# Edge messages of a graph network in batches of five tiles instead of four, with begun sums made at one go

## The chip, the cores and the metric

The kernel runs on one core of a Trainium2 chip. The metric is the device time of one execution in microseconds (us). The core has five engines that run side by side, each through its own list of instructions in order: TensorE (PE; its weight loads are shown apart as PEld), VectorE (DVE), ScalarE (ACT), GpSimd (POOL) and SyncE (SP, which issues transfers). Matmuls write to PSUM, eight banks of 512 floats in each of 128 partitions; everything else works in the larger SBUF.

## What is computed

One block of a graph network on 1250 nodes of 512 floats (three vector components of 128 channels and 128 scalars) with 40000 edges, a residual and a layernorm:

```python
s_j = silu(x[src][:, 384:] @ W1 + b1) @ W3 + b3
edge_basis = rbf(r) * cutoff(r) @ W2 + b2          # 20 radial functions of the edge's length
s1, s2, s3 = split(s_j * edge_basis)
v_msg = v_j * s1[:, :, None] + s3[:, :, None] * edge_attr1[:, None, :]
x = x + segment_sum(concat(v_msg, s2), dst)        # first half
v, dot, s1, s3 = per_node(x, U, V, Wu1, Wu2)      # norms and a small network
x = x + segment_sum(concat(v * s1, dot + s3)[src], dst)   # second half
out = layernorm(x_in + x)
```

The edges come sorted by destination; source rows have to be gathered.

## The kernel before, in words

The nodes form NB = 10 blocks of 128 rows. A first part (to about 38 us) loads everything, runs the first two layers for each node and writes a table of 640 floats per node to DRAM (`table1`). Then follows the edge loop, in which nearly all the time goes.

**Tiles and batches.** 40000 edges are 79 chunks of 512, and each chunk has four tiles of 128 edges. Four chunks make a group `g` (20 groups); a batch is tile `i` of each of the four chunks of a group. So there are NT = 80 batches: 76 of four tiles, then of 3, 2, 2 and 2, 313 tiles in all. The loop runs over steps `t`, one batch each.

**A step.** DVE runs `messages(t)`: two multiplies of the gathered rows by the edge factors, in place (L938, on 4 x 256 elements, and L940, on 4 x 384), then `make_hot` (L870: a one-hot matrix of destinations) and `make_spread` (L881: the same times the edge's direction), and `make_pair` (L958, for the count of links). Both hot and spread read four columns that the factors' matmul carries along, so L881 is the last reader of the factor banks. PE adds the messages of the batch before (`add_messages(t - 1)`, L974 and L980, 4 + 12 matmuls), counts its links (`count_links`, L1003), and makes the factors of the next batch (`edge_factors(t + 1)`, L928). Each tile's factors are a matmul over 25 rows at row 32 j of the array, j being the tile's chunk in the group; the trace shows two per tile. They go to `eb`, one set of four PSUM banks, which is made new only when L881 has read the last factors. POOL runs `gather(t + 3)` (L769), one indirect DMA of 128 rows for each tile, the first of them behind `edge_factors(t + 1)` by a dependency put there by hand. The rows have five rooms of four tiles, taken in turn: three in the tile that the profile calls `more`, two in `nodes`.

**Second half.** The other work is hung between these steps by tables: `first`, `early`, `late`, `mid`, `dve` and `amid` list tasks by step and rank, and `run(when, step)` issues them at fixed places of the step: `early` on PE ahead of the next factors, `late` behind them, `amid` on DVE ahead of the pair, `dve` at the step's end. Every eight steps or so two groups close, and a block of nodes passes through its second half with short products that all use one PSUM bank, `work` (`ps_work`, one buffer). The second segment sum uses a matrix of link counts (`cast`) and the finished rows, split in two parts (`upper`, `lower`). As rows of early blocks are there long before the last, ten partial sums ("chains", `begin_out`, L1378) and a last one are begun during the loop in a bank of their own, `begun`: from step 24 on, one pair of products at a time, in slots of `early` and `late`, then copied by ACT (L1397) and sent to DRAM. So the eight banks are four of `eb`, and `work`, `agg`, `adj` and `begun`. After the loop the sums are completed and normalized.

The schedule is manual: instructions run on each engine in the order in which the code issues them.

Of the kernel before, what the change touches and what calls it, by code (L numbers as in the profile page):

```python
# [21 lines left out]
P = 128  # L22
C = 128
# [23 lines left out]
PACK = 4096.0  # L47

# [16 lines left out]
def gnn_resnorm(  # L65
# [43 lines left out]
    )  # L109
    sh.n_nodes, sh.width, sh.n_edges, sh.NB, sh.tail = n_nodes, width, n_edges, NB, tail  # L110
# [40 lines left out]
    def load(engine, ap, shape, name):  # L151
        t = const.tile(shape, F32, name=name)
        engine.dma_start(t, ap)
        return t
# [15 lines left out]
    sh.nodes = const.tile([P, NB * width], F32, name="nodes")  # L170
# [14 lines left out]
    size = CPG * (V + 2 * C)  # L185
    sh.more = const.tile([P, 3 * size], F32, name="more")
# [14 lines left out]
    sh.w1_sb = load(nc.sync, w1, [C, C], "w1_sb")  # L201
# [9 lines left out]
    sh.w3_sb = load(nc.sync, w3, [C, V], "w3_sb")  # L211
# [407 lines left out]
def windowed(tc, sh):  # L619
# [36 lines left out]
    NT = len(batches)  # L656

# [3 lines left out]
    def runs(g, i):  # L661

        out = []
        for j in tiles(g, i):
            if out and lanes(g, i, out[-1][-1]) == lanes(g, i, j):
                out[-1].append(j)
            else:
                out.append([j])
        return [(slice(js[0], js[-1] + 1), len(js), lanes(g, i, js[0])) for js in out]

# [12 lines left out]
    with tc.tile_pool(  # L683
# [5 lines left out]
        turn = pool.tile([P, 2, EPG, N_RBF], F32, name="turn", bufs=1)  # L689
        upper, lower = (  # L690
            pool.tile([P, NB, width], F32R, name=name, bufs=1) for name in ("upper", "lower")
        )

# [67 lines left out]
        rooms = itertools.cycle(sh.rooms)  # L761

        def gather(t, behind=None):

            g, i = batches[t]
            rows_t = next(rooms)
            for j in tiles(g, i):
                n = lanes(g, i, j)
                got = nc.gpsimd.indirect_dma_start(  # L769
                    out=rows_t[:n, j, :],  # L770
# [3 lines left out]
                        ap=sh.src_i[:n, g, i * CPG + j : i * CPG + j + 1], axis=0  # L774
                    ),
                )
                if behind is not None and j == 0:
# [4 lines left out]
            clear_rest(t, rows_t, nc.gpsimd)  # L782
            rows_of[t] = rows_t
# [63 lines left out]
        def clear_rest(t, tile, engine=nc.vector):  # L847
            g, i = batches[t]
            for j in tiles(g, i):
                m = lanes(g, i, j)  # L850
                if m < P:
                    engine.memset(tile[m:, j], 0.0)

        def carried(t, js, m):

            g, i = batches[t]
            if g == 0:
                return sh.carried[:m, g, i * CPG + js.start : i * CPG + js.stop, :]
            return factors_of(t, js)[:m, :, V : V + CARRY]

        def make_hot(t):

            g, i = batches[t]
            hots[t] = pool.tile([P, CPG, WIN], F32, name="hot", bufs=3)
            spread[t] = pool.tile([P, CPG, 3, WIN], F32, name="spread", bufs=3)
            clear_rest(t, hots[t])
            clear_rest(t, spread[t])
            for js, n, m in runs(g, i):
                shape = [m, n, WIN]
                nc.vector.tensor_tensor(  # L870
                    hots[t][:m, js, :],
                    lane[:m, None, :WIN].to_broadcast(shape),
                    carried(t, js, m)[:, :, 3:].to_broadcast(shape),
# [3 lines left out]
        def make_spread(t):  # L877
            g, i = batches[t]
            for js, n, m in runs(g, i):
                shape = [m, n, 3, WIN]  # L880
                nc.vector.tensor_mul(  # L881
                    spread[t][:m, js],
                    hots[t][:m, js, None, :].to_broadcast(shape),
                    carried(t, js, m)[:, :, :3, None].to_broadcast(shape),
                )
# [23 lines left out]
        made_in = {}  # L909
# [10 lines left out]
        def factors_of(t, js):  # L920

            return made_in[t][:, js]

        def edge_factors(t):
            g, i = batches[t]
            for j in tiles(g, i):
                rows = slice(j * FEAT, j * FEAT + N_RBF + 1 + CARRY)
                made = nc.tensor.matmul(  # L928
                    made_in[t][:, j, : V + CARRY], turned[g][rows, i, :], sh.w2_sb[rows, :],
# [4 lines left out]
        def messages(t):  # L934
            g, i = batches[t]
            msg = rows_of.pop(t)
            for js, n, m in runs(g, i):
                nc.vector.tensor_mul(msg[:m, js, V:], msg[:m, js, V:], factors_of(t, js)[:m, :, C:V])  # L938
            for js, n, m in runs(g, i):
                nc.vector.tensor_mul(  # L940
                    msg[:m, js, :V].rearrange("p t (k c) -> p t k c", k=3),
                    msg[:m, js, :V].rearrange("p t (k c) -> p t k c", k=3),
                    factors_of(t, js)[:m, :, None, :C].to_broadcast([m, n, 3, C]),
                )
            make_hot(t)
            make_spread(t)
            run(amid, t)
            make_pair(t)
            msgs[t] = msg
# [18 lines left out]
        def add_messages(t):  # L968
# [3 lines left out]
            agg, msg, js = aggs[g], msgs.pop(t), tiles(g, i)  # L972
            for j in js:
                nc.tensor.matmul(  # L974
                    agg[j * WIN : (j + 1) * WIN, :], hots[t][:, j, :],
                    msg[:, j, :width], start=(i == 0), stop=False, skip_group_check=True,
                )
            for c in range(3):
                for j in js:
# [1194 lines left out]
```

## Time and profile before

| | |
|---|---|
| runs | 478.65, 477.8, 480.88 us (median 478.65) |
| profiled execution | 480.96 us, of which the span of the trace is 479.2 |
| mean granted TensorE clock | 0.957 |
| busy: PE, DVE, ACT, POOL | 402.6, 427.8, 375.3, 334.9 us |
| first gather starts, last gather starts | 26.35, 426.96 us |

Times in the trace are microseconds from the start of the span. A row of a group gives the line, the engine and operation, the tile written and those read, partitions x elements of each, the count, and behind the bar the busy time, the mean in ns and the engine's idle time before these instructions with what ended it. "issue" is idle time in which the engine waited for nothing that the profile shows. A row of the timeline gives the start, the duration, and in brackets the idle time before it and its releaser; neighbours of one kind are drawn together (x8). A row of a window gives its length and the busy time and count for PE, PEld, DVE, ACT and POOL, then the granted clock, the DMA share and GB/s.

### The profile page before, as it was taken

Reading aid. Unit: us, or ns where it says so; the run is one execution under the profiler, and the core shown is the slowest. Engines: PE = TensorE matmul, PEld = TensorE weight load, DVE = VectorE, ACT = ScalarE, POOL = GpSimd, SP = SyncE. Lnnn points to the kernel's source line nnn. Section 1 sums busy time; section 2 is a strip of 40 time slices with the busy share of each in tenths; the row PEclk is TensorE's granted clock in tenths of the full one; section 3 lists DMA queues with packets and bytes.
Section 4 is the critical chain, followed back from the end, with each engine's and each line's share of the span. In section 5 each row is a group of like instructions: output and inputs, shape, how many; then the busy total and the mean of one; then the engine's idle time right before and its main releaser. Section 6 shows DMA issues by size and latency. Waiting matters only on the chain. (4 is left out here: it accounts for less than half of the span.)

```text
span 479.2 us, 11259 instructions
## 1 busy us (share of the span) xinstructions
PE 402.6 (84%) x4259; PEld 229.3 (48%) x4259; DVE 427.8 (89%) x675; ACT 375.3 (78%) x971; POOL 334.9 (70%) x364
## 2 busy tenths in 40 slices
PE   8645586878879778798889888989999999999992
PEld 6322243445445345444435544555555655555782
DVE  6569899999999899999999999999999999978584
ACT  4377846689869968877977897799899889967672
POOL 9267777777777777777777777777777777771530
PEclk9857979899999999989989999999999999999998
DMA  8887888788888888888888988888888888879024
GB/s 238 301 247 253 254 265 271 240 279 262 281 254 272 289 259 275 270 269 255 280 276 255 293 267 280 266 291 287 287 275 293 265 284 291 280 242 319 4 71 151
DMA packets 37810, 123.29 MB, mean 257 GB/s; under 512 B 7124, under 2 KB 9782, under 8 KB 37746
## 3 DMA queue, kind: packets, MB, share of 16 engines
q0 software_dynamic: 25568, 104.34, 69.0%
q1 hardware_dynamic: 10834, 17.35, 10.6%
q10 hardware_dynamic: 1344, 0.79, 0.5%
q8 instruction: 35, 0.57, 0.5%
q14 instruction: 29, 0.24, 0.2%
HBM read 112.94 MB, written 9.51 MB: 256 GB/s over the span
## 5 line engine op out<-in xcount | busy, mean ns | idle before, releaser
L769 POOL DMA_INDIRECT more<-table,src_i x189 | 184.6, 977 | 66.3 <-issue 48.1
L769 POOL DMA_INDIRECT nodes<-table,src_i x124 | 119.8, 966 | 37.8 <-issue 33.2
L903 ACT ACTIVATE one<-one,weight,src_f 128x128 f16<-128x128 f16 x313 | 128.5, 482 | 0.2
L928 PE MATMUL eb<-w_sb,basis_t 25*128 25x388 f32 x614 | 74.1, 551 | 54.3 <-DVE spread L881 43.9
L893 ACT ACTIVATE one<-number,low 128x128 f16<-128x128 f16 x313 | 99.8, 392 | 11.2 <-PE adj L1003 11.2
L940 DVE TENSOR_TENSOR more<-more,eb 128x1536 f32<-128x1536 f32 (+2 forms) x48 | 81.8, 1705 | 0.0
L938 DVE TENSOR_TENSOR more<-more,eb 128x1024 f32<-128x1024 f32 (+2 forms) x48 | 57.0, 1190 | 15.0 <-PE eb L928 8.2
L928 PEld LDWEIGHTS eb<-w_sb,basis_t 25*128 25x128 f32 x614 | 24.7, 187 | 76.5 <-DVE spread L881 63.7
L974 PE MATMUL agg<-more,hot 128*32 128x512 f32 x378 | 52.8, 624 | 0.0
L940 DVE TENSOR_TENSOR nodes<-nodes,eb 128x1536 f32<-128x1536 f32 x30 | 52.4, 1747 | 0.0
L980 PEld LDWEIGHTS agg<-more,spread 128*32 128x32 f32 x1134 | 33.5, 111 | 30.2 <-issue 29.6
L938 DVE TENSOR_TENSOR nodes<-nodes,eb 128x1024 f32<-128x1024 f32 x30 | 36.5, 1216 | 6.9 <-PE eb L928 4.0
L881 DVE TENSOR_TENSOR spread<-hot,eb 128x384 f32<-128x384 f32 (+1 forms) x74 | 40.4, 547 | 2.5
L980 PE MATMUL agg<-more,spread 128*32 128x128 f32 x1134 | 40.2, 273 | 0.0
L958 DVE TENSOR_TENSOR pair<-number,column 128x640 f16<-128x640 f16 (+1 forms) x81 | 38.5, 476 | 0.0
L1003 PE MATMUL adj<-pair,one 128*128 128x160 f16 x313 | 35.4, 235 | 0.3 <-DVE basis L827 0.3
L974 PE MATMUL agg<-nodes,hot 128*32 128x512 f32 x248 | 34.9, 619 | 0.0
L980 PEld LDWEIGHTS agg<-nodes,spread 128*32 128x32 f32 x744 | 22.7, 112 | 20.0 <-issue 19.6
L1003 PEld LDWEIGHTS <-one 128*128 128x128 f16 x313 | 21.6, 100 | 16.0 <-issue 13.5
L845 ACT COPY basis_t<-work 128x512 f32<-128x512 f32 x20 | 11.6, 580 | 22.5 <-PE work L840 22.5
L1378 PE MATMUL begun<-upper,cast 128*128 128x512 f32 x57 | 27.8, 487 | 0.0
L980 PE MATMUL agg<-nodes,spread 128*32 128x128 f32 x744 | 27.5, 277 | 0.0
(299 smaller groups left out, 697.3 us busy)
## 6 DMA issues: line engine op xcount, KB each, us to landing
table<-more SPq DMA_DIRECT2D x10, 320.0 KB
more<-table,src_i POOLq DMA_INDIRECT x189, 4.2
spilled<-begun SPq DMA_DIRECT2D x10, 256.0 KB
more<-spilled SPq DMA_DIRECT2D x2, 1280.0 KB
node_x<-in_x_dram SPq DMA_DIRECT2D x35, 64.0 KB
nodes<-table,src_i POOLq DMA_INDIRECT x124, 4.2
out_dram<-more SPq DMA_DIRECT2D x7, 256.0 KB
nodes<-in_x_dram POOLq DMA_DIRECT2D x2, 768.0 KB
```

The lines of the kernel that those rows point to most:

```text
L769: got = nc.gpsimd.indirect_dma_start(out=rows_t[:n, j, :], out_offset=None, in_=sh.table1, in_offset=bass.IndirectOffsetOnAxis(ap=sh.src_i ...
L881: nc.vector.tensor_mul(spread[t][:m, js], hots[t][:m, js, None, :].to_broadcast(shape), carried(t, js, m)[:, :, :3, None].to_broadcast(shape),
L893: nc.scalar.activation(onehots[t][:, j, :], number[:, :P], AF.Abs, bias=low[:, e : e + 1])
L903: nc.scalar.activation(one, one, AF.Relu, scale=less[:, e : e + 1], bias=worth[:, e : e + 1])
L928: made = nc.tensor.matmul(made_in[t][:, j, : V + CARRY], turned[g][rows, i, :], sh.w2_sb[rows, :], start=True, stop=True,)
L938: nc.vector.tensor_mul(msg[:m, js, V:], msg[:m, js, V:], factors_of(t, js)[:m, :, C:V])
L940: nc.vector.tensor_mul(msg[:m, js, :V].rearrange("p t (k c) -> p t k c", k=3), msg[:m, js, :V].rearrange("p t (k c) -> p t k c", k=3), fac ...
L958: nc.vector.tensor_tensor(pair[:m, js, :].rearrange("p t (l h) -> p t l h", h=2), number[:m, : PARTS * WIN].rearrange("p (l h) -> p l h", ...
L974: nc.tensor.matmul(agg[j * WIN : (j + 1) * WIN, :], hots[t][:, j, :], msg[:, j, :width], start=(i == 0), stop=False, skip_group_check=True,)
L980: nc.tensor.matmul(agg[j * WIN : (j + 1) * WIN, c * C : (c + 1) * C], spread[t][:, j, c, :], msg[:, j, width:], start=False, stop=(i == la ...
L1003: nc.tensor.matmul(to[:, :, at : at + WIN], one[:m, j, :], pair[:m, j, :].rearrange("e (p n) -> e p n", n=WIN), start=(i == 0 and j == js[ ...
L1378: nc.tensor.matmul(acc, casts[a, b], rows[:, a, :], start=(start and a == first and k == 0), stop=(stop and a == end - 1 and k == 1),)
```

## The change

**Packs of five.** Factors, gathers, multiplies, hot and spread go by packs of five consecutive tiles of the batches' order: 60 packs of five, one of four, then 3, 2, 2 and 2 (65 packs for 80 batches). The steps stay: each adds one batch of four, counts its links, makes its pair. In step s the pack `step_of(s)` = ceil(4 s / 5) is worked if it is new, so four of five steps have a pack, and steps 5, 10, 15, ... have none. `eb` has five banks. A pack's fifth tile has the same j as its first, so it uses the same 32 rows of PE's array.

**Rows.** `more` and `nodes` become one tile `both` of 20 slots, and five slots more (`spare_slots`) make 25, so that gathers run three packs, 15 tiles, ahead instead of three batches, 12 tiles. To have that memory, the last two blocks' `upper` and `lower` and `cast_last` get a home only at step 76 (`late_homes`), in the place of `spare_slots`, and `w1`, `w3` lie in a pool of the first part.

**Begun sums.** The fifth bank is that of `begun`. Each chain is now made in one run in the `work` bank and copied by ACT at once, at a fixed step ahead of the factors; the last one is made at step 75 behind the factors, and copied there rather than at step 78. At step 76 the five banks become four of two "halves" and a late `begun` bank (`ps_late`).

**Moved.** The pieces that make the radial functions (`make_turns`, `make_basis`, `turn_basis`, `bring_fades`) come one or two steps earlier, all four pieces of the first at step 0; at the start, `turn_attr` uses the banks `agg`, `work` and `adj`.

On DVE, before, one step (batch 22, and the first multiply of 23), a pack of four instructions in each step:

```order
L938 TENSOR_TENSOR more<-more,eb_386 128x4x256
L940 TENSOR_TENSOR more<-more,eb_386 128x4x384
L870 TENSOR_TENSOR hot<-lane,eb_386 128x128
L881 TENSOR_TENSOR spread<-hot,eb_386 128x384
L958 TENSOR_TENSOR pair<-number,column 128x640
L801 TENSOR_SCALAR h_t<-turn 128x320
L804 TENSOR_TENSOR turn<-turn,h_t 128x320
L938 TENSOR_TENSOR nodes<-nodes,eb_386 128x4x256
```

and now, from pack 16 to the first multiply of pack 17 (steps 19 and 20):

```order
L999 TENSOR_TENSOR both<-both,eb_389 128x5x256
L1001 TENSOR_TENSOR both<-both,eb_389 128x5x384
L932 TENSOR_TENSOR hot<-lane,eb_389 128x160
L942 TENSOR_TENSOR spread<-hot,eb_389 128x480
L854 TENSOR_TENSOR turn<-ratio,adj 128x640
L1017 TENSOR_TENSOR pair<-number,column 128x640
L1365 TENSOR_TENSOR lower<-x_979,upper 128x512
L1017 TENSOR_TENSOR pair<-number,column 128x640
L863 TENSOR_SCALAR h_t<-turn 128x320
L866 TENSOR_TENSOR turn<-turn,h_t 128x320
L999 TENSOR_TENSOR both<-both,eb_389 128x5x256
```

The instructions of a pack have 5/4 of the elements; between packs 16 and 17 there are the pairs and other tasks of two steps, and between other packs those of one.

On PE, before, from the factors of batch 36 to those of batch 37 (the left-out rows are three more of L1003's pairs):

```order
L928 MATMUL eb_386<-w_sb,basis_t 128x388 x4
L974 MATMUL agg<-more,hot 32x512 x4
L980 MATMUL agg<-more,spread 32x128 x12
L1003 LDWEIGHTS one
L1003 MATMUL adj<-pair,one 128x5x32
...
L1138 MATMUL work<-u_sb,x_t 128x128 x3
L1378 MATMUL begun<-upper,cast 128x512
L1378 MATMUL begun<-lower,cast 128x512
L928 MATMUL eb_386<-w_sb,basis_t 128x388 x4
```

and now from the factors of pack 29 to those of pack 30, in steps 34 to 36 (left out: more of L1064):

```order
L990 MATMUL eb_389<-w_sb,basis_t 128x388 x5
L1034 MATMUL agg<-both,hot 32x512 x4
L1041 MATMUL agg<-both,spread 32x128 x12
L1188 MATMUL work<-ident,x_2345 128x128 x4
L1064 LDWEIGHTS one
L1064 MATMUL adj<-pair,one 128x5x32
...
L1034 MATMUL agg<-both,hot 32x512 x4
L1041 MATMUL agg<-both,spread 32x128 x12
...
L1199 MATMUL work<-u_sb,x_t 128x128 x3
L990 MATMUL eb_389<-w_sb,basis_t 128x388 x5
```

The additions and link counts of two steps, and the second half's products that belong there, stand between two sets of factors; in three of four places it is those of one step.

A begun sum on PE now, chain (4, 0, 4) at step 46: left out are more of L1064 and three more pairs like the one shown. The rows behind L1064 are all of the chain, up to the factors of pack 38:

```order
L1226 MATMUL work<-ident,square 128x128 x3
L1034 MATMUL agg<-both,hot 32x512 x4
L1041 MATMUL agg<-both,spread 32x128 x12
L1064 LDWEIGHTS one
L1064 MATMUL adj<-pair,one 128x5x32
...
L1442 MATMUL work<-upper,cast 128x512
L1442 MATMUL work<-lower,cast 128x512
...
L990 MATMUL eb_389<-w_sb,basis_t 128x388 x5
```

Before, such pairs stood singly, as the one in the row of batch 36 above.

The diff, cut to what the prediction speaks of:

```diff
+    tile_order = [(t, j) for t in range(NT) for j in tiles(*batches[t])]
+    place_of = {at: n for n, at in enumerate(tile_order)}
+    joint = place_of[NT - SHORT - 1, 0]
+    packs = [list(range(n, n + PACK_OF)) for n in range(0, joint, PACK_OF)]
+    packs += [[place_of[t, j] for j in tiles(*batches[t])] for t in range(NT - SHORT - 1, NT)]
...
+    def step_of(s):
+        return -(-4 * s // 5) if s < NT - SHORT else s - NT + NK
...
-        def edge_factors(t):
-            g, i = batches[t]
-            for j in tiles(g, i):
+        def edge_factors(k):
+            for q, n in enumerate(packs[k]):
+                t, j = tile_order[n]
+                g, i = batches[t]
                 rows = slice(j * FEAT, j * FEAT + N_RBF + 1 + CARRY)
                 made = nc.tensor.matmul(
-                    made_in[t][:, j, : V + CARRY], turned[g][rows, i, :], sh.w2_sb[rows, :],
+                    made_in[k][:, q, : V + CARRY], turned[g][rows, i, :], sh.w2_sb[rows, :],
                     start=True, stop=True,
                 )
...
-        def begin_out(chain, a):
+        def begin_out(chain):
             b, begin, end = chain
-            if a == begin:
-                accs[b] = ps_sum.tile([P, BANK], F32, name="begun")
-            products(accs[b], b, a, a + 1, a == begin, a == end - 1)
-            if a == end - 1 and b < NB - 2:
-                copy_begun(b, chain)
+            acc = work()
+            products(acc, b, begin, end, True, True)
+            copy_begun(b, acc, chain)
...
+        steps_of = {
+            (4, 0, 4): 46, (0, 0, 4): 48, (3, 0, 4): 51, (5, 0, 5): 53, (2, 0, 5): 56,
+            (6, 0, 6): 61, (1, 0, 6): 63, (7, 0, 7): 71, (0, 4, 7): 70, (3, 4, 7): 68,
+        }
...
+            at(early, step, 8, begin_out, chain)
...
-        at(early, NT - 2, 7, copy_begun, NB - 2)
+        at(late, NT - 5, 9, begin_out, last_chain)
...
-        [eb] = new_banks("eb", [CPG])
+        [eb] = new_banks("eb", [PACK_OF])
...
+            k = step_of(s)
+            new = k not in begun_steps
+            begun_steps.add(k)
+            if new and k < NK:
+                messages(k)
+            if s < NT:
+                run(amid, s)
+                make_pair(s)
...
             if 1 <= s <= NT:
                 add_messages(s - 1)
                 if s not in behind:
                     count_links(s - 1)
             run(early, s)
+            if new and k + 1 < NK - 2:
+                made = edge_factors(k + 1)
...
+            if new and k + ahead < NK:
+                gather(k + ahead, made if k + ahead < NK - 2 else None)
```

More of the change, by code (lines that the diff above doesn't have):

```diff
@@ L47 @@
 PACK = 4096.0
+PACK_OF = 5
 REC = 8
@@ L169, in gnn_resnorm @@
     nc.vector.memset(bias_f, 0.0)
-    sh.nodes = const.tile([P, NB * width], F32, name="nodes")
+    size = CPG * (V + 2 * C)
+    both = const.tile([P, 5 * size], F32, name="both")
+    sh.more, sh.nodes = both[:, : 3 * size], both[:, 3 * size :]
+    sh.slots = both.rearrange("p (t f) -> p t f", f=V + 2 * C)
     sh.xt = sh.nodes.rearrange("p (b f) -> p b f", f=width)
@@ L845, in turn_basis, with clear_rest @@
             nc.scalar.copy(turned[g].rearrange("p i e -> p (i e)"), tp)
[L847 to L850, printed above, removed]
+        def clear_rest(k, tile, engine=nc.vector):
+            for q, n in enumerate(packs[k]):
+                m = lanes_of(n)
                 if m < P:
[L852 to L868, printed above, removed]
+                    engine.memset(tile[m:, q], 0.0)
+        kept_apart = sh.carried.rearrange("p g t c -> p (g t) c")
+        def carried(k, qs, m):
+            first = packs[k][0]
+            if first < EPG:
+                return kept_apart[:m, first + qs.start : first + qs.stop, :]
+            return factors_of(k, qs)[:m, :, V : V + CARRY]
@@ L1067, in sum_block @@
                 blks[b] = (
-                    work() if b < NB - 1 else ps_sum.tile([P, BANK], F32, name="begun")
+                    work() if b < NB - 1 else ps_late[0].tile([P, BANK], F32, name="begun")
                 )
@@ L1580, in windowed @@
         assert len(row_order) == 10
-        for b, _, end in sorted(chains):
+        for b, _, end in row_order:
             begun[b] = end
-        units = [(chain, a) for chain in chains for a in range(*chain[1:])]
-        slots = (
-            (0, early), (0, late), (1, late), (2, early), (2, late), (3, early), (3, late),
-            (4, early), (4, late), (5, late), (6, late), (7, early), (7, late), (7, late),
-        )
-        after = 0
-        free_slots = [(8 * c + step, when) for c in range(3, NB) for step, when in slots]
@@ new lines, in windowed @@
+        begun_steps = set()
+        for s in range(max(*first, *early, *late, *dve, *mid) + 1):
+            k = step_of(s)
[6 more added lines that the diff above has]
+                make_pair(s)
+            if s == NT - SHORT:
+                late_homes()
+                assert all(len(packs[n]) == CPG // 2 for n in range(NK - 3, NK))
+                factor_banks.close()
+                ps_late.append(
+                    banks.enter_context(tc.tile_pool(name="ps_late", bufs=1, space=PSUM))
+                )
+                made_in[NK - 3], made_in[NK - 2] = new_banks("halves", [CPG // 2] * 2)
+                made_in[NK - 1] = made_in[NK - 3]
+            if s == NT - 1:
+                out_banks.update(zip(in_factors, new_banks("out", [1] * CPG), strict=True))
+            run(first, s)
+            if 1 <= s <= NT:
+                add_messages(s - 1)
+                if s not in behind:
+                    count_links(s - 1)
+            run(early, s)
+            if new and k + 1 < NK - 2:
+                made = edge_factors(k + 1)
+            if new and k + 1 in (NK - 3, NK - 2):
+                edge_factors(k + 2)
+            if new and k + ahead < NK:
+                gather(k + ahead, made if k + ahead < NK - 2 else None)
+            if s in behind:
+                count_links(s - 1)
+            run(mid, s)
+            run(late, s)
+            run(dve, s)
```

267 lines of the change are left out of this document (140 added, 127 removed).

## The prediction

> **What bounds the kernel now.** I read the page first, then the waits of POOL and DVE, then single instructions in the edge loop.
>
> ```profile
> span 479.2 us, 11259 instructions
> PE 402.6 (84%) x4259; PEld 229.3 (48%) x4259; DVE 427.8 (89%) x675; ACT 375.3 (78%) x971; POOL 334.9 (70%) x364
> L769 POOL DMA_INDIRECT more<-table,src_i x189 | 184.6, 977 | 66.3 <-issue 48.1
> L769 POOL DMA_INDIRECT nodes<-table,src_i x124 | 119.8, 966 | 37.8 <-issue 33.2
> ```
> ```profile
> POOL more L769 <- issue: 48.1, 158, 0.3
> POOL nodes L769 <- issue: 33.2, 109, 0.3
> ```
> ```profile
> 26.35 1.09 POOL L769 DMA_INDIRECT more<-table,src_i  x1 [7.61 <-DVE turn L792]
> ...
> 426.96 0.95 POOL L769 DMA_INDIRECT nodes<-table,src_i  x1 [0.30 <-issue]
> ```
>
> POOL shows 70%, yet it sets the pace. 313 gathers start between 26.35 and 426.96: 400.6/312 = 1.284 us each. One takes 0.95 to 0.98, and ahead of 267 of them stand 0.3 us that no other engine caused. So 0.95 + 0.30 = 1.25 is the least a gather takes, and a batch of four cannot come faster than 5.0 us.
>
> ```profile
> 82.94 1.22 DVE L938 TENSOR_TENSOR nodes<-nodes,eb 128x1024 f32<-128x1024 f32 x1 [0.65 <-PE eb L928]
> ```
> ```profile
> 415.51 1.22 DVE L938 TENSOR_TENSOR nodes<-nodes,eb 128x1024 f32<-128x1024 f32 x1
> ```
> ```profile
> 82.93:415.51 332.58, 294.25 (x3383) 162.06 (x3383) 314.99 (x449) 282.56 (x743) 252.60 (x261) 0.98 0.86 274
> ```
>
> The two multiplies open batches 9 and 74: 65 steps in 332.57 us, 5.117 us each, or 25.6 for the five steps that will hold four packs. The third row is that stretch by engine (PE, PEld, DVE, ACT, POOL): DVE works 314.99/65 = 4.85 per step, PE 294.25/65 = 4.53. Three engines lie within 0.6 us of the pace. What takes over once the pattern changes is therefore the question, and it is decided by the loop between DVE and PE over the one set of factor banks:
>
> ```profile
> 262.31 1.21 DVE L938 TENSOR_TENSOR nodes<-nodes,eb 128x1024 f32<-128x1024 f32 x1
> 263.44 1.74 DVE L940 TENSOR_TENSOR nodes<-nodes,eb 128x1536 f32<-128x1536 f32 x1
> 265.10 0.28 DVE L870 TENSOR_TENSOR hot<-lane,eb 128x128 f32<-128x128 f32 x1
> 265.42 0.56 DVE L881 TENSOR_TENSOR spread<-hot,eb 128x384 f32<-128x384 f32 x1
> 265.89 0.48 DVE L958 TENSOR_TENSOR pair<-number,column 128x640 f16<-128x640 f16 x1
> 267.03 1.22 DVE L938 TENSOR_TENSOR more<-more,eb 128x1024 f32<-128x1024 f32 x1 [0.66 <-PE eb L928]
> ```
> ```profile
> 266.03 0.93 PE L928 MATMUL eb<-w_sb,basis_t 25*128 25x388 f32 x8 [0.84 <-DVE spread L881]
> ```
>
> Four tiles' messages take from 262.31 to 265.98, 3.67 us. The spread is the last reader of the banks; the next factors run 0.05 after its end, for 0.93, and the next multiply starts 1.05 after the spread. DVE covers that gap with other work, 4.85 - 3.67 = 1.18 us per step on average; where the step has only a pair, as here, it idles (0.66).
>
> ```profile
> DVE more L938 <- PE eb L928: 8.2, 12, 2.7
> DVE more L938 <- DMA more<-table,src_i: 4.1, 5, 1.4
> DVE nodes L938 <- PE eb L928: 4.0, 8, 0.7
> ```
>
> The loop now costs DVE 8.2 + 4.0 = 12.2 us in all, the gathers about 5.
>
> **The change part by part. Fewer DVE instructions.** Fifteen groups of L938, L940, L870, L881 go away.
>
> ```profile
> L940 DVE TENSOR_TENSOR more<-more,eb 128x1536 f32<-128x1536 f32 x46 | 80.4, 1747 | 0.0
> L938 DVE TENSOR_TENSOR more<-more,eb 128x1024 f32<-128x1024 f32 x46 | 56.0, 1218 | 12.3 <-PE eb L928 5.5 <-DMA more<-table,src_i 4.1 <-issue 2.7
> ```
>
> (1747 - 1218)/512 = 1.033 ns per element. Four tiles are 3072 elements, 3.17 us, so 0.5 of the 3.67 is fixed. Five tiles: 3.67 + 768 x 1.033 ns = 4.46 us. Four packs for five batches save 5 x 3.67 - 4 x 4.46 = 0.5 per five steps, 7.5 us in 15 cycles, if DVE sets the pace. The Trainium skill's "VectorE: DVE Perf Modes" (The TRN2 errata) has a fixed term of about 151 cycles per instruction, 0.157 us, which agrees with a single one here (1218 - 1058 = 160 ns); as an estimate from that page the 60 removed instructions would be 9.4 us rather than 7.5, since it leaves out that the next one starts 0.08 early (262.31 to 263.44 is 1.13).
>
> **The fifth tile's factors.** Tile j's matmuls work on rows 32j to 32j + 24, so four tiles lie beside each other, and a pack's fifth uses the rows of its first. The tail has such a case: two batches of two tiles, each pair of row groups used twice.
>
> ```profile
> 430.78 1.57 PE L928 MATMUL halves<-w_sb,basis_t 25*128 25x388 f32 x8 [0.17 <-DVE spread L881]
> 432.28 0.33 PE L1179 MATMUL work<-ident,s 128*128 128x128 f32 x1
> ```
>
> Eight matmuls as before, 1.57 instead of 0.93; PE's next work starts after 1.50. The fifth costs 0.64; bounds are 0 (it slips in beside the others) and 0.93 (a round by itself). I take 0.64, the row with the same reuse. A multiply can then start 1.69 after the spread, not 1.05. With a cover of 1.18 on average, most gaps between packs (43 of 60 by the new order) are too short, and a single-step interval is about 1.74 + 4.46 = 6.2 us.
>
> **Four bursts in five steps.** Three intervals between bursts hold one step of PE's other work, the fourth two, since the step without a new pack still adds, counts, and does its early and late work. PE runs in order: all of it stands ahead of the next burst.
>
> ```profile
> 100.00:260.00 160.00, 133.90 (x1605) 73.79 (x1597) 151.03 (x215) 132.14 (x349) 121.91 (x126) 0.98 0.86 270
> 275.00:415.00 140.00, 132.47 (x1483) 73.64 (x1476) 133.72 (x194) 124.19 (x324) 106.45 (x111) 1.00 0.87 282
> ```
> ```profile
> PEld eb L928 <- DVE spread L881: 43.8, 39, 2.4
> ```
> ```profile
> PEld eb L928 <- DVE spread L881: 9.2, 19, 0.9
> ```
>
> 133.90 over 160/5.117 = 31.3 steps is 4.28; less 0.93, PE's other work is 3.35 per step early; 132.47 over 27.4 steps gives 3.9 late. The two wait rows (82.9 to 300, and 300 to 415) bound it below: (217.1 - 43.8)/42.4 - 0.93 = 3.2 and (115 - 9.2)/22.5 - 0.93 = 3.8. I take 3.35 and 3.9. They also say that PE has slack to wait in early, and hardly any late. The double interval is then 1.5 + 2 x 3.35 = 8.2 early, 1.5 + 7.8 = 9.3 late, while DVE has 2 x 1.18 + 4.46 = 6.8 to do: here DVE waits, and in the three others PE does (1.5 + 3.9 = 5.4 < 6.2). Neither can lend its slack, because the banks are single.
>
> Cycle: 3 x 6.2 + 8.2 = 26.8 early, 3 x 6.2 + 9.3 = 27.9 late, against 25.6. Nine cycles (steps 1 to 45) x 1.2 = +11; six (46 to 75) x 2.3 = +14. With the lower work, 3.2 and 3.8: +8 and +13.
>
> **Begun sums at one go.**
>
> ```profile
> 302.67 0.48 PE L1378 MATMUL begun<-upper,cast 128*128 128x512 f32 x1
> 302.99 0.40 PE L1378 MATMUL begun<-lower,cast 128*128 128x512 f32 x1
> 303.32 0.93 PE L928 MATMUL eb<-w_sb,basis_t 25*128 25x388 f32 x8
> ```
> ```profile
> 453.09 0.40 PE L1378 MATMUL out<-upper,cast 128*128 128x512 f32 x1
> 453.33 0.40 PE L1378 MATMUL out<-lower,cast 128*128 128x512 f32 x1
> 453.56 0.40 PE L1378 MATMUL agg<-upper,cast 128*128 128x512 f32 x1
> ```
>
> A pair by itself takes 0.65, in a row 0.47. The 11 chains have 52 pairs: between 0 (they stood in rows already) and 41 x 0.18 = 7; I take -2, since only intervals that PE bounds return it. Against it, 6 to 14 products (1.4 to 3.3 us) now stand in one step. Those of steps 46, 51, 56, 61, 70 and 71 lie in double intervals and are in the 9.3; the four of 48, 53, 63 and 68 (9 products on average, 2.1) come on top of 3.9 less the 0.6 per step that the pieces took (47 pairs x 0.65 over some 50 steps), so that a single needs 1.5 + 3.3 + 2.1 = 6.9 against 6.2: +2 in all (0 to 4). Their copy out of the bank is under rivals.
>
> **Gathers.** Still 313. They start 15 tiles ahead instead of 12, and only each fifth waits on the factors; 20 x 1.284 = 25.7 is hidden under 26.8 and 27.9. DVE's waits of 5 us on them vanish into the longer cycle: 0. If the loop were shorter than I think, this pace would return as the bound.
>
> **Start and end.** The first pack waits for one more gather, +1.3, of which some lies under preparation: +1. In the tail the last begun copy moves forward:
>
> ```profile
> 439.42 1.79 POOL L1414 TENSOR_TENSOR begun<-begun,h_t 128x512 f32<-128x512 f32 x1 [7.72 <-ACT begun L1397]
> 444.02 1.59 POOL L1369 CAST cast_last<-counts 128x1280 fp32r<-128x1280 f16 x2 [2.81 <-ACT counts L1043]
> ```
>
> POOL no longer waits 7.7, but its next work waits for the last counts until 444.02 anyway: -1 (0 to -2). Moved turns, loads and late tiles keep their work, in steps with room: 0.
>
> **Sum.** 11 + 14 - 2 + 2 + 1 - 1 = +25 us. The profiled execution took 480.96 (span 479.2), so it would be 506; it lies 0.5% above the median 478.65, from which the forecast is **504 us**.
>
> **Rivals. A, POOL's pace stays the bound.** If the fifth tile costs PE next to nothing, a multiply comes 1.05 after the spread: singles 1.2 + 4.46 = 5.7, doubles 0.9 + 6.7 = 7.6 to 8.7, cycles 24.7 and 25.8; the gathers' 25.7 rules. The time is 477 to 482, no change. For it: POOL's rows. Against: the 1.57.
>
> **B, faster.** The same, and PE's double interval stays under DVE's because its work shrinks by the joined chains; the deeper look-ahead then lets gathers go at 1.25 rather than 1.284, 313 x 0.034 = -10, and DVE, with 7.5 less, follows: with the tail -11, 468; half of it 472. For it: many gathers are spaced exactly 1.25 in the rows above. Against: the same row of 1.57, and PE's 4.84 per step late.
>
> **C, slower still, the work bank.** A begun chain now holds the single `work` bank from its first product until ACT has copied it, and nothing that passes through `work` can begin meanwhile.
>
> ```profile
> 438.76 0.58 ACT L1397 COPY begun<-begun 128x512 f32<-128x512 f32 x1
> ```
>
> ACT is 78% busy, so copy and queue are some 0.6 to 0.8; 11 times is up to 9 us if a work product stands next on PE: 512. The Trainium skill's "Perfetto Trace Analysis" (Optimizing Tensor Performance, Matmuls) has a rule against this edit: independent groups of matmuls should rotate through different PSUM banks, so that one's evacuation overlaps the next one's products. No row of before shows it for this bank.
>
> **How the numbers follow.** The forecast (two-step interval on PE, one-step interval on factors, some 490 to 512) has 0.62, C 0.11, A 0.13, B 0.14. About 1%, 5 us, is what a measurement of this kernel can tell from no change. Faster is B, 0.14; same is A, 0.13; slower the rest, 0.73. The fifth tile's bounds carry the range: at 0.3 us the cycles are 25.9 and 27.1, about 490; at 0.93 singles are 6.5 and both cycles 1.2 more than mine, 518. With half of A it is 478 to 518.
>
> **What would show it.** Right: the factor matmuls of a pack (x10) take about 1.57; DVE's first multiply waits on them some 40 us in all instead of 12; every fourth interval between multiplies is 8 to 9 us, the others near 6.2; POOL's gathers are no longer spaced by 0.30 "issue", but wait on PE's factors; batches 9 to 74 take some 22 us more than 332.6. Wrong: bursts near 1.0, or double intervals under 7.5; then POOL's 0.30 before each gather remains, and A or B holds. For C, PE waits on ACT's begun copy.

## The result, and the profile after

The changed kernel takes 569.09 us (565.46 to 573.24, four runs) against 478.5 before: a ratio of 1.186 (1.181 to 1.192). It is slower, as forecast, but by 90 us where 25 were forecast, and far outside the range. The profiled execution took 565.46 us. Its page:

```profile
span 563.6 us, 11219 instructions
PE 454.8 (81%) x4259; PEld 265.4 (47%) x4259; DVE 424.5 (75%) x615; ACT 389.4 (69%) x979; POOL 334.8 (59%) x364
PEclk9758789888988889899798898989879989989998
```

DVE has its 60 instructions less and is busy 3 us less. PE makes the same 4259 matmuls and is busy 52 us longer. The row PEclk (granted clock in tenths, 40 slices) is at 8 in many slices inside the loop, where before it stood at 9 with few exceptions. The waits, by engine and line (us in total, times, longest):

```profile
DVE both L999 <- PE eb L990: 57.3, 25, 10.3
...
DVE spare_slots L999 <- PE eb L990: 9.7, 7, 4.4
```
```profile
POOL both L831 <- PE eb L990: 67.0, 20, 12.3
POOL both L831 <- issue: 65.8, 208, 2.7
```
```profile
PE eb L990 <- DVE spread L942: 45.5, 36, 3.3
PE eb L990 <- DVE both L1001: 11.9, 4, 7.3
PE work L902 <- ACT s L1296: 8.9, 8, 2.4
```
```profile
ACT one L954 <- PE adj L1064: 44.3, 15, 5.0
```

DVE waits 67 us for factors (12 before), POOL 84 for the same burst, ACT 44 for PE, and PE for both. No engine is the bound: each waits in turn for another. PE's wait at L902 for ACT's copy `s` is new; before, the same matmul (L840) waited now and then for other copies of ACT, never for this one.

Where it went, by multiplies that open packs 8, 36 and 60 (tiles 40, 180, 300):

```profile
88.95 1.49 DVE L999 TENSOR_TENSOR both<-both,eb 128x1280 f32<-128x1280 f32 x1 [1.25 <-PE eb L990]
```
```profile
295.77 1.49 DVE L999 TENSOR_TENSOR both<-both,eb 128x1280 f32<-128x1280 f32 x1
```
```profile
498.07 1.21 DVE L999 TENSOR_TENSOR both<-both,eb 128x1024 f32<-128x1024 f32 x1
```
```profile
88.95:498.07 409.12, 339.03 (x3385) 193.51 (x3389) 312.75 (x397) 297.53 (x754) 251.17 (x261) 0.92 0.72 224
```

These 260 tiles, 65 steps, take 409.12 us; 65 steps took 332.57 before. So 76.5 us of the span's 84.4 arise in the loop. A cycle of five steps is 29.5 us over the seven cycles to pack 36 (206.8/7) and 33.7 over the six behind it (202.3/6), against 25.6 before and 26.8 and 27.9 forecast. The granted clock over the stretch is 0.92 (0.98 before). In this trace the granted clock is either 1.00 or 0.50 at a time, so 0.92 means, as an estimate, 0.16 x 409 = 65 us at half clock and some 33 us of PE's work lost, against 13 us and 7 before.

One cycle shows how it comes about. PE, DVE, ACT and POOL around the empty step, in four views of the timeline:

```profile
122.47 1.56 PE L990 MATMUL eb<-w_sb,basis_t 25*128 25x388 f32 x10
...
126.99 0.44 PE L1064 MATMUL adj<-pair,one 128*128 128x160 f16 x4 [0.67 <-DVE basis L889]
128.30 0.22 PE L1274 MATMUL work<-bias,ones_r 65*128 65x128 bf16 x1 [0.87 <-ACT h_t L1269]
128.35 0.44 PE L1275 MATMUL work<-wu_sb,h_t 128*128 128x128 f32 x2
131.15 0.66 PE L902 MATMUL work<-ident,basis 128*128 128x128 f32 x4 [2.36 <-ACT s L1296]
131.74 1.94 PE L1034 MATMUL agg<-both,hot 128*32 128x512 f32 x8
133.44 1.51 PE L1041 MATMUL agg<-both,spread 128*32 128x128 f32 x24
134.88 0.54 PE L1064 MATMUL adj<-pair,one 128*128 128x160 f16 x4
135.35 1.57 PE L990 MATMUL eb<-w_sb,basis_t 25*128 25x388 f32 x10
```
```profile
117.53 1.49 DVE L999 TENSOR_TENSOR both<-both,eb 128x1280 f32<-128x1280 f32 x1
...
126.45 0.49 DVE L889 TENSOR_TENSOR basis<-turn,adj 128x320 f32<-128x320 f32 x1 [4.05 <-ACT turn L868]
...
127.25 1.48 DVE L999 TENSOR_TENSOR both<-both,eb 128x1280 f32<-128x1280 f32 x1
...
136.96 1.49 DVE L999 TENSOR_TENSOR spare_slots<-spare_slots,eb 128x1280 f32<-128x1280 f32 x1 [4.36 <-PE eb L990]
```
```profile
128.15 1.26 ACT L954 ACTIVATE one<-number,low 128x128 f16<-128x128 f16 x4
129.31 1.64 ACT L964 ACTIVATE one<-one,weight,src_f 128x128 f16<-128x128 f16 x4
130.85 0.24 ACT L1296 COPY s<-work 128x128 f32<-128x128 f32 x1
```
```profile
137.19 0.95 POOL L831 DMA_INDIRECT both<-table,src_i  x1 [6.39 <-PE eb L990]
```

Read it from the top. ACT comes late to the turn, so DVE's basis waits 4.05 and PE's link count behind it 0.67. L1275 leaves its result in the work bank at 128.8, but ACT has two groups of one-hot rows (128.15 to 130.9) ahead of the copy L1296. L902 needs the same bank and now stands straight behind: PE waits 2.36. The next additions run at half speed (1.94 and 1.51, else 1.06 and 0.84). From burst to burst it is 12.9 us where the forecast had 8.2: 3.9 of waits, 1.6 at half clock. DVE waits 4.36 for it, POOL 6.39.

The clock over two windows of PE's work, ahead of the wait and behind it:

```profile
124.00:128.00 4.00, 2.76 (x41) 1.73 (x41) 1.55 (x3) 3.94 (x6) 3.09 (x4) 1.00 0.90 294
131.70:135.40 3.70, 3.70 (x41) 1.77 (x40) 0.89 (x3) 2.14 (x6) 0.00 (x0) 0.54 0.35 114
```

Another way into it needs no bank: ahead of the empty step PE has slack, waits 2.33 us for a spread, and starts the two steps' work at half clock.

```profile
154.03 1.56 PE L990 MATMUL eb<-w_sb,basis_t 25*128 25x388 f32 x10 [2.33 <-DVE spread L942]
...
156.17 1.93 PE L1034 MATMUL agg<-both,hot 128*32 128x512 f32 x8
```

The Trainium skill's page "TensorE: Matmul & The Clock Gate" (Part 1: The HAM clock gate) states that the array falls to half clock after an idle window of some 3.4 us that runs freely; here waits of 2.3 us were enough, as the window may also hold the thinner work beside them.

In the tail, step 75 has no new pack either, and the last chain's ten products stand in it ahead of the last factors; POOL then waits for the last counts:

```profile
510.91 0.50 PE L1442 MATMUL work<-upper,cast 128*128 128x512 f32 x1 [0.96 <-ACT vv L1218]
...
515.47 1.57 PE L990 MATMUL halves<-w_sb,basis_t 25*128 25x388 f32 x8
```
```profile
POOL cast_last L1433 <- ACT counts L1104: 12.6, 1, 12.6
```

From tile 300's multiply to the end it is 65.5 us, against 58.7 before (420.50 to 479.2): 6.8 lost.

### The profile page after: what moved, and what is told of

It reads as the page before. It is cut to its first block, busy times and chain, and to the rows that moved or that the text cites. A ratio compares the mean times of both kernels' runs of the same rounds, so it can differ in the third digit from the quotient of the medians.

```text
span 563.6 us, 11219 instructions
## 1 busy us (share of the span) xinstructions
PE 454.8 (81%) x4259; PEld 265.4 (47%) x4259; DVE 424.5 (75%) x615; ACT 389.4 (69%) x979; POOL 334.8 (59%) x364
## 4 chain that ended last, share of the span: by engine, by line
DVE 35%; PE 31%; ACT 13%; issue 10%; POOL 5%; DMA 4%; DVEq 0%; SPq 0%; POOLq 0%
PE eb L990 12%; DVE both L1001 10%; DVE both L999 7%; PE agg L1034 5%; ACT one L964 4%; DVE spread L942 4%; DVE spare_slots L1001 3%; PE agg L1041 3%; PE work L1442 3%; DVE spare_slots L999 2%; POOL both L831 2%; PE adj L1064 2%; ACT one L954 2%; DMA both<-in_x_dram 2%; DVE hot L932 2%
## 5 line engine op out<-in xcount | busy, mean ns | idle before, releaser
L831 POOL DMA_INDIRECT both<-table,src_i x253 | 247.1, 977 | 147.4 <-PE eb L990 67.0
L990 PE MATMUL eb<-w_sb,basis_t 25*128 25x388 f32 x614 | 100.0, 544 | 57.5 <-DVE spread L942 45.5
L954 ACT ACTIVATE one<-number,low 128x128 f16<-128x128 f16 x313 | 99.8, 391 | 44.3 <-PE adj L1064 44.3
L999 DVE TENSOR_TENSOR both<-both,eb 128x1280 f32<-128x1280 f32 (+3 forms) x51 | 73.5, 1444 | 63.2 <-PE eb L990 57.3
L1001 DVE TENSOR_TENSOR both<-both,eb 128x1920 f32<-128x1920 f32 (+3 forms) x51 | 106.2, 2084 | 0.0
L1034 PE MATMUL agg<-both,hot 128*32 128x512 f32 x506 | 92.3, 699 | 0.0
L1041 PEld LDWEIGHTS agg<-both,spread 128*32 128x32 f32 x1518 | 57.7, 122 | 48.9 <-issue 47.2
L831 POOL DMA_INDIRECT spare_slots<-table,src_i x60 | 57.7, 962 | 33.9 <-PE eb L990 16.8
L1041 PE MATMUL agg<-both,spread 128*32 128x128 f32 x1518 | 69.9, 297 | 0.0
L1064 PE MATMUL adj<-pair,one 128*128 128x160 f16 x313 | 38.0, 247 | 1.6 <-DVE basis L889 1.5
L942 DVE TENSOR_TENSOR spread<-hot,eb 128x480 f32<-128x480 f32 (+3 forms) x59 | 37.7, 640 | 1.9
L1064 PEld LDWEIGHTS <-one 128*128 128x128 f16 x313 | 23.4, 104 | 20.8 <-issue 19.2
L1034 PE MATMUL agg<-spare_slots,hot 128*32 128x512 f32 x120 | 32.3, 749 | 0.0
L902 PE MATMUL work<-ident,basis 128*128 128x128 f32 x80 | 15.3, 322 | 17.0 <-ACT s L1296 8.9
L999 DVE TENSOR_TENSOR spare_slots<-spare_slots,eb 128x1280 f32<-128x1280 f32 x12 | 17.8, 1486 | 12.6 <-PE eb L990 9.7
```

The costliest lines, as they stand in the source:

```text
L831: got = nc.gpsimd.indirect_dma_start(out=rows_k[:m, q, :], out_offset=None, in_=sh.table1, in_offset=bass.IndirectOffsetOnAxis(ap=sh.src_i ...
L942: nc.vector.tensor_mul(spread[k][:m, qs], hots[k][:m, qs, None, :].to_broadcast(shape), carried(k, qs, m)[:, :, :3, None].to_broadcast(shape),
L954: nc.scalar.activation(onehots[t][:, j, :], number[:, :P], AF.Abs, bias=low[:, e : e + 1])
L990: made = nc.tensor.matmul(made_in[k][:, q, : V + CARRY], turned[g][rows, i, :], sh.w2_sb[rows, :], start=True, stop=True,)
L999: nc.vector.tensor_mul(msg[:m, qs, V:], msg[:m, qs, V:], factors_of(k, qs)[:m, :, C:V])
L1001: nc.vector.tensor_mul(msg[:m, qs, :V].rearrange("p t (k c) -> p t k c", k=3), msg[:m, qs, :V].rearrange("p t (k c) -> p t k c", k=3), fac ...
```

## The experiments

Theories: **(1)** packs of five as forecast: the fifth tile's factors and the step without a pack; **(2)** the work bank: chains hold it, and the radial pieces, moved earlier, put L902 straight behind L1275; **(3)** PE's clock, halved by the waits; **(4)** ACT held up by three buffers of one-hot rows. Chips differ: on three of those used the kernel before took 560 to 566 us, not 478 to 480, so every number is set against before, or the changed kernel, on the same kind of chip. Where an expectation below gives microseconds for a chip as that of the result and the run came on one of the three others, only its ratio can be compared.

**The changed kernel, packs of four, and packs of four with a bank for the chains** (one chip, before 480.2 us). Packs of four, besides slots that fit:

```diff
-PACK_OF = 5
+PACK_OF = 4
-        return -(-4 * s // 5) if s < NT - SHORT else s - NT + NK
+        return s
```
and for the second the bank that is left free:
```diff
-            acc = work()
+            acc = ps_chain.tile([P, BANK], F32, name="begun")
```

> The changed kernel itself, beside the three others on this chip: on the chip of the result its ratio to before was 1.19 (1.18 to 1.19). Chips seem to differ in how often TensorE's clock is halved, so the others are read against this run.

> The changed kernel with packs of four, every step with a pack; begun chains in the work bank, earlier turns, late tiles and spare slots stay. If packs of five carry the loss: 1.00 to 1.03 of before. If the work bank and the earlier turns carry it: over 1.08.

> The same with packs of four, and the bank that this leaves free given to the begun chains, still each at one go: only the hold on the work bank is taken away. If that hold carries what packs of four still lose, it is 1.00 to 1.02 of before and 3% or more below packs4b; if the lump of 6 to 14 products ahead of the factors carries it, it is within 1% of packs4b.

Measured: the changed kernel 568.6 us, 1.187 (1.171 to 1.203); packs of four 528.9, 1.104 (1.090 to 1.118); with the chains' own bank 513.7, 1.073 (1.059 to 1.087). So packs of five cost 39.7 us, the chains' hold of the work bank 15.2, and 33.5 belong to what is left, with four tiles in every step as before. Neither expectation came out cleanly: packs of four stayed over 1.08, the branch of the work bank and the turns, yet gave back 39.7 us; and the chains' own bank gave back 2.9%, near the 3% expected, but stayed at 1.073, not 1.02. In that last kernel most intervals between multiplies are 4.7 to 5.7 us, as before or shorter; but each eighth, from batch 16 to 17, 24 to 25 and so on up to 56, is 8.1 to 10.5. It is the step in which L902 stands first:

```profile
166.93 1.12 PE L902 MATMUL work<-ident,basis 128*128 128x128 f32 x4 [2.36 <-ACT s L1296]
167.97 1.93 PE L1034 MATMUL agg<-spare_slots,hot 128*32 128x512 f32 x8
169.68 1.50 PE L1041 MATMUL agg<-spare_slots,spread 128*32 128x128 f32 x24
```
```profile
163.80 1.22 DVE L999 TENSOR_TENSOR both<-both,eb 128x1024 f32<-128x1024 f32 x1 [0.26 <-PE eb L990]
...
172.58 1.22 DVE L999 TENSOR_TENSOR both<-both,eb 128x1024 f32<-128x1024 f32 x1 [4.24 <-PE eb L990]
```

The wait, then half clock, then DVE idle 4.24: 8.78 instead of some 5.1. Six such intervals (mean 9.0) are about 3.9 us too long each, 23 of the 33.5; two of the six, at steps 48 and 56, hold a begun chain as well. Four other steps with a chain, 46, 61, 63 and 71, take 6.5 to 7.6, some 8 us more together. That is read from the trace; the runs on this place below are from other chips.

**PE kept busier** (same chip). The first products of the additions once more with zero weights in three of five steps:

```diff
+            if t + 1 < 46 and (t + 1) % 5 > 1:
+                for j in js:
+                    k, q = pack_of[place_of[t, j]]
+                    nc.tensor.matmul(
+                        agg[j * WIN : (j + 1) * WIN, :], no_hot,
+                        msgs[k][:, q, :width], start=False, stop=False, skip_group_check=True,
+                    )
```

> The changed kernel with more work: up to step 45, in the steps whose interval is a single one, the first four products of the additions are made once more with weights of zero (0.9 us of PE in 27 steps), which leaves the sums as they are. If TensorE's clock is halved because PE idles 2 us or more ahead of the factors, this shortens the idle time, halved stretches go and the kernel gets faster by 10 us or more. If PE's work by itself is the bound, it gets slower by up to 24 us; if the idle time is just slack, nothing changes.

Measured: 569.2 us, 1.188 (1.176 to 1.201), no change against 568.6. Its waits show that slack was filled, yet not at L902 (here L904):

```profile
PE eb L992 <- DVE spread L944: 32.0, 28, 3.4
...
PE work L904 <- ACT s L1305: 8.7, 8, 2.4
```

PE's waits for the spread fell from 45.5 to 32.0 us, but the clock of the same packs is 0.93 where it was 0.92, and the waits for ACT are as they were. So 27 x 0.9 us of work in single intervals cost nothing: they are slack, as forecast. What half clock costs by itself stays open, as this did not take it away.

**The work bank, on the other chips.** Two kernels: the kernel before with the change's radial pieces alone, and the changed kernel with packs of four, the chains' bank, and the pieces as before. Of the second's edit, the lines that put the pieces back (the first makes the same move the other way):

```diff
-                at(amid, base - 5, 4, make_turns, g, n, 0)
...
-                at(first, base, 1, turn_basis, g)
+                at(amid, base - 3, 4, make_turns, g, n, 0)
...
+            at(first, base + 3, 1, turn_basis, g)
```

> The kernel before with one edit of the change alone: the pieces of the radial functions at the changed kernel's steps, so that L840 (there L902) stands straight behind the layer's product in the work bank every eighth step. If that place costs 3 to 4 us in each of eight cycles, half clock behind it included: 500 to 512 us on a chip as that of the result. If the gathers' pace hides it: within 1%.

> Packs of four, begun chains at one go in their own bank, radial pieces at the steps of before; late tiles, spare slots and the new start stay. With the place of L902 as the cause of what packs4_bank loses (34 us): 478 to 490 us. If the chains at one go or the start cost it: over 500.

The first run of each had this on record:

> The kernel before with one edit of the change alone: the pieces of the radial functions one to three steps earlier, as in the changed kernel (the first group's as before). If L902's place behind L1275's product costs 3 to 4 us in each of eight cycles, half clock behind it included, this is 25 to 32 us over before (1.05 to 1.07). If PE's wait there is slack that the gathers' pace hides, nothing changes (within 1%).

> Packs of four, begun chains in their own bank, and now the radial functions' pieces (turns, basis, L902) at the steps of before; chains at one go, late tiles, spare slots and the new start stay. In packs4_bank every eighth interval, the one in which L902 stands straight behind L1275's product, is 8 to 9 us instead of 5. If that place costs the rest, this is 1.00 to 1.02 of before (478 to 490); if the chains at one go or the new start cost it, it stays over 1.05.

Measured: 574.0 us, 1.015 (1.010 to 1.020), and 572.1, 1.011 (1.007 to 1.016), before 565.6 there; a first run of each (in the one of the pieces alone a group's basis is overwritten early) gave 1.019 and 1.019. So chains at one go, late tiles, spare slots and the new start cost 1 to 2% there, and the pieces' earlier places, that of L902 among them, cost 1.5% by themselves, between the two branches expected (1.05 to 1.07, or under 1%). In the trace of the pieces alone each eighth interval from batch 16 to 48 takes 7.0 to 8.0 us where most take 6.1 to 6.2; that would be some 7 of the 8.4 us, but there is no trace of before from these chips to set beside it. Neither can be carried over in us: on these chips the loop of factors is slower. Here a burst in the second kernel and the multiply that waits for it:

```profile
150.43 0.93 PE L990 MATMUL eb<-w_sb,basis_t 25*128 25x388 f32 x8 [0.73 <-DVE hot L932]
```
```profile
152.93 1.22 DVE L999 TENSOR_TENSOR both<-both,eb 128x1024 f32<-128x1024 f32 x1 [1.12 <-PE adj L1064]
```

2.50 us from the burst's start to the multiply, where before had 1.00 (266.03 to 267.03): most steps there are 6.1 to 6.2 us, and a wait elsewhere is partly covered by that. Packs of four without the chains' bank ran on such a chip too:

> The changed kernel with packs of four tiles, so that every step has a pack again and the factors take four banks; the begun chains at one go in the work bank, the earlier turns, the late tiles and the spare slots stay. If the loss comes from packs of five (the step without a pack, the fifth tile), it is back near before: 478 to 490 us. If it comes from the work bank (chains, and the turned basis straight behind the layer's product), most of it stays: 510 us or more.

It measured 624.8 us, 1.116 (1.106 to 1.125), before 560.3. The rows of some of its last batches are overwritten early, and its last steps (11 to 14 us) were long for that, so it adds nothing to the run of packs of four above.

**The turned basis under packs of five** (one chip, before 560.5).

```diff
-                at(first, base, 1, turn_basis, g)
+                at(first, base, 1, turned.__setitem__, g, None)
```

> The changed kernel once more, beside the next run. On a chip as that of the result its ratio to before is 1.19; on the chips where before takes 560 us, the runs with a small edit of it were at 1.19 to 1.28, so 1.20 to 1.25 there.

> The changed kernel without L902's matmuls and their copy for the groups 3, 5, ... 19 (work left out: the basis of the group before is used again), beside the changed kernel on the same chip. If L902's place behind L1275's product in the work bank carries the 34 us that packs of four with their own begun bank lose, it carries them here too: 5% or more below the changed kernel. If under packs of five PE waits at the next place instead (the step without a pack stalls by itself), under 2%.

The second kernel's two earlier runs:

> The changed kernel, packs of five, without L902's matmuls and their copy for the groups 3, 5, ... 19 (the basis of the group before is used again: work left out). What remains up to step 45, where no begun chain stands yet, is the cost of packs of five: by the prediction's sum a cycle of five steps would be 26.8 us there. If the hold of the work bank was the reason for the 29.5 us measured, it comes near 27, and the whole is 530 to 545; if the step without a pack itself stalls, it stays at 29 or more and the whole over 555.

> The changed kernel, packs of five, without L902's matmuls and their copy for the groups 3, 5, ... 19 (work left out: the basis of the group before is used again). If the hold of the work bank there was the reason why two intervals in each cycle take 18 us, a cycle before step 45 comes near the forecast's 26.8 and the whole is 525 to 540. If the step without a pack itself stalls, it stays at 29 and over 555.

Measured: 684.2 us, 1.221 (1.215 to 1.227), and without the turn 679.4, 1.211 (1.205 to 1.218): 0.7% less; the earlier runs gave 1.210 and 1.208 on such chips. The other branch holds there: with packs of five, taking the product at L902 away leaves the time nearly as it is, and PE waits at the next place (48.1 us for the spread, 40.0 with the turn). For the chip of the result that isn't shown.

**The turned basis behind the additions instead.**

```diff
-                at(first, base, 1, turn_basis, g)
+                at(early, base, 5.2, turn_basis, g)
```

> The changed kernel with one task moved: the basis of a group is turned (L902) after the additions and link counts of its step instead of ahead of them, so that PE no longer asks for the work bank right behind the product that ACT has yet to copy out of it. If PE's wait of 8.9 us there and the slower matmuls after it cost time on the path, some 15 to 25 us come back (545 to 555). If the two steps of work between factors set the pace, under 5 us.

Measured: 716.5 us, 1.279 (1.266 to 1.293), worse than the changed kernel's 1.221 on such chips. The wait moved:

```profile
PE work L1131 <- ACT basis_t L907: 32.8, 7, 7.3
```

L1131, the next block's sum, needs the bank next, and PE waits there for ACT's copy of the basis. My reading, that the additions would cover it, was wrong: at this place too the product has a neighbour in the bank.

**The fifth tile.** Edit: `if k and q == 4: continue` in the loop over a pack's tiles in `edge_factors`.

> The changed kernel without the factor matmuls of each pack's fifth tile (its bank keeps old factors, all other work stays). Burst 0.93 instead of 1.57. If the fifth tile's reuse of rows carries the loss, three single intervals of each cycle lose 0.6 and the double one too: 60 x 0.6 = 36 us, to 533. If the double interval carries it, the singles still lose 0.6 (45 x 0.6 = 27) but the intervals around the empty step stay at 15 us or more for two, and the time is 540 to 550.

> The changed kernel without the factor matmuls of each pack's fifth tile from the second pack on (old factors stay in its bank; work left out), on a chip as that of the result. Singles 5.5 to 5.6 instead of 6.13 where nothing else binds, 25 to 36 us less in all (533 to 545) if the fifth tile's reuse of rows is on the path as forecast; under 15 us less if the intervals around the step without a pack take it up.

> The changed kernel without the factor matmuls of each pack's fifth tile from the second pack on (work left out). If the fifth tile's reuse of its rows is on the path as forecast, singles are 5.5 instead of 6.13 and the whole is 530 to 545. Under 15 us less if the intervals around the step without a pack take it up.

Measured, in this order: 670.4, 676.1 and 675.2 us, 1.197 (1.188 to 1.206), 1.200 (1.195 to 1.205) and 1.194 (1.180 to 1.208). Against 1.221 it is 2 to 3 points, some 9 to 15 us, less than the 25 that were expected if the fifth tile was on the path in all the singles. Nearly nine tenths of the loss there remain without any fifth tile.

**Four buffers of one-hot rows**: `bufs=3` to `bufs=4`.

> The changed kernel with four buffers instead of three for the one-hot rows of links (L954), so that ACT need not wait for PE's link counts. If ACT's 44 us of waiting there makes it late for PE, 20 us or more come back (under 550). If ACT only waits because PE itself is late, nothing changes: 563 to 570.

Measured: 686.3 us, 1.225 (1.215 to 1.236), the same as 1.221. ACT's wait at L954, 37 to 44 us in the changed kernel, is down to 1.1 us in this trace, and the time is the same, so it was slack: the theory is out.

## Why the prediction was wrong

**Right.** POOL gave up the pace to the loop between DVE and PE. The fifth tile's burst is 1.56 to 1.57 as in the tail's row, and a single interval is 6.13 (forecast 6.2; 111.40 to 117.53 is one). Fewer DVE instructions bought nothing, and singles have slack on PE.

**The step that failed: "Four bursts in five steps".** It took PE's busy time per step, 3.35 and 3.9, twice, plus a burst: 8.2 and 9.3. Measured: 29.5 and 33.7 per cycle for 26.8 and 27.9, 7 x 2.7 + 6 x 5.8 = 54 us above the forecast's loop. From burst to burst, the trace has 39 of these 54 in the thirteen double intervals, while 25 of the 39 singles take 6.1 to 6.2. The seven early doubles take 10.1 on average for 8.2, with PE busy for 8.6 of it; the six late ones 13.7 for 9.3, with PE busy for 11.7. Here the late one that holds no begun chain, and the longest:

```profile
439.11:448.43 9.32, 9.18 (x98) 5.10 (x98) 7.38 (x12) 8.45 (x24) 6.39 (x7) 1.00 0.86 263
399.35:417.95 18.60, 14.98 (x111) 9.37 (x111) 8.87 (x14) 9.57 (x25) 6.48 (x7) 0.74 0.49 154
```
```profile
412.53 0.80 PE L1442 MATMUL work<-upper,cast 128*128 128x512 f32 x1 [1.72 <-ACT basis_t L907]
```

Two things were wrong in the sum. *Waits and the clock were left out.* Busy time adds only if nothing in the two steps waits, but each step passes several products through one bank, PE to ACT and back, with ACT's own rows in between. Before, as I read it, POOL's pace left time for this within each step; with two steps' hand-overs in one interval, PE waits, and seven of the thirteen intervals also have a stretch at half clock. *The chains were put "in the 9.3", but they are not in it.* The 3.9 per step holds about 0.6 of single pairs, 1.2 in two steps, while the chains' products take 2.1 to 5.4 us in each of the five late doubles that hold any, 18.7 in all. The sixth measured 9.3, as forecast. Packs of five alone measured 39.7 where the sum had 11 + 14 + 1. How much half clock costs by itself stays open.

**Moved work "in steps with room: 0"** failed as well. It was put at nothing without a reason: the order showed L902 next to L1275, but I never asked who had to empty the bank between them. In the kernel with packs of four, the intervals with that neighbourhood are the long ones (about 23 of its 33.5 us by the trace). The three terms (packs of five, the chains' hold, the moved pieces) aren't independent, so these numbers aren't a sum that would hold in another kernel.

**Rival C** was there, but priced as copies alone, up to 9 us, and as a case apart. With packs of four, its chains measured 15.2, on top of the rest. **The clock** was in no term: 0.98 before looked like a constant, but in these traces it falls behind PE's longer waits, of which before had few.

**The tail** lost 6.8 where 1 was to be gained: the last chain of ten products at step 75 stands on PE ahead of the last factors (burst at 515.47), and POOL's cast waits 12.6 for the counts, not 2.8. The chain's place isn't enough to explain it: packs of four with the chains' bank have the same ten products there and take 58.7 from tile 300's multiply to the end (455.01 to 513.7), as before. In the changed kernel the interval is a double one, with half clock in it.

**The signs listed** were half right: DVE's waits 67 us (forecast 40); batches 9 to 74 take 76.5 us more (forecast 22); in several cycles two in four intervals between multiplies, not one, are 8 us or more, since DVE's two steps lie one pack ahead of PE's (packs 16 to 17 and factors 29 to 30 in the rows of the change), which the prediction took for one interval; POOL waits 84 us for factors, yet 259 gathers still stand at 0.30, in bursts between long waits.

**Two sums of the range** don't come out. At 0.3 us for the fifth tile the prediction's own terms give cycles of 25.4 and 26.5, not 25.9 and 27.1, and at 0.93, 1.2 more in 15 cycles is 522, not 518. The measured 569 lies far outside either way.

## What to carry over

When an edit concentrates two steps' work into one interval, count the hand-overs through single buffers in it, and what each partner has queued ahead, not only busy time; and add up the work of that very interval, not twice the average step. Ask of each task that is moved which task last used its buffer and who empties that. A bound that hides slack for others (here POOL's pace) also hides their waits; once the pace is gone, they show all together.

## What the runs showed of the hardware

In the changed kernel's loop each of the twelve waits of 2.2 to 3.4 us on PE leads into 3.4 or 6.8 us at a granted clock of 0.50 (0.54 in the window shown, which reaches past the end), with 1.94 for additions that else take 1.06. Shorter waits do it at times: in packs of four with the chains' bank, 1.81 us did (burst at 186.95, clock 0.50 from 188.4). And the same program differs by 17% between chips (480 and 560 us), with a longer way from PE's burst to DVE's multiply (2.50 and 1.00 in the rows shown), though DVE's own instructions take the same 1.22; why isn't settled.
